# End of layer 1's cross attention: three operations change engine or place

## The chip, the cores and the metric

One Trainium2 chip; the kernel runs on one of its cores. The metric is the device time of one execution in microseconds (us). The core's engines work side by side, each on a queue of its own: PE (TensorE: matrix products and transposes through PSUM), DVE (VectorE), ACT (ScalarE), POOL (GpSimd) and SP, which here only issues transfers. An engine takes its instructions in order; where one needs the result of another engine, it waits, and everything behind it in that queue waits too.

## The reference

Two decoder layers on 32 sequences of 100 tokens of 256 values in float32, each layer with self attention, cross attention to a context of 361 positions of 192 values, and a feed-forward part. The change lies where layer 1's cross attention ends and its mixture of experts begins:

```python
# cross attention of layer 1
q = xn @ Wq
kv = context @ Wkv
...
dots = jnp.where(mask, dots, -jnp.inf)
attn = jax.nn.softmax(dots, axis=-1)
out = jnp.einsum('bhnm,bhmd->bhnd', attn, v)
...
return out @ Wo + bo
# experts of layer 1, on x_flat = rows of _layernorm(x)
shared = jnp.einsum('td,dh->th', jax.nn.silu(shared), shared_w2.T)
gate_logits = x_flat @ gate_w.T
top_k_gates, top_k_idx = jax.lax.top_k(gate_logits, TOP_K)
...
expert_out = jnp.einsum('teh,edh->ted', jax.nn.silu(h), experts_w2)
selected = jnp.einsum('ted,te->td', expert_out, gates)
return (shared + selected).reshape(B, S, D)
x = x + _L1_ffn_ref(_layernorm(x, axis=-1), ...)
```

## The kernel before

The 32 sequences are taken in 8 groups of 4 (`NG`, `G`). The cross attention works in 128 units (`NU`): unit u is one sequence with four of its 16 heads. For a unit, `scores` makes the products of queries and keys, DVE adds the mask and takes the row's extreme, `exponentials` lets ACT evaluate Exp (one instruction of 100x361 a head, with the row sums), and `divided` takes the reciprocal of the four row sums on DVE and multiplies all four heads' weights by it on POOL (100x1444 in one instruction, line 2369). `turn_weights` transposes the weights on PE in three chunks of the context positions, four heads a chunk; ACT copies the first and the third chunk from PSUM and DVE the second. `sums` multiplies them with the values on PE, and DVE copies the result into `oT`.

The order is written out by hand: `two_turns(n)` runs units n and n+1 in the stage of `turn_weights` and `sums`, while later units' values, keys, scores and exponentials are put between. Within `in_order()` the queues of PE, DVE, ACT and POOL follow that order exactly; SP's does not. Two units ahead, `half_of(n)` divides unit n+1. For the last pair, n = 126, nothing is left to put between: unit 127 is divided in `half_of(126)`, and then follow both units' transposes, both units' sums, and `finish` of the last group (the output projection of `oT`, bias on DVE for one half at line 147 and on ACT for the other at line 142, transposes back at line 2426, the residual sum on DVE at line 2433, transfer of the new rows to `x_dram`).

`gating` is the way of one group's rows into the experts, in parts: part 0 the statistics of the layer norm on DVE with a power and a product on POOL (lines 168 to 183, in `stats`), part 1 the norm itself in place, four ACT instructions of 100x256 (`scaled`, line 199), part 2 the transposes of the normed rows (line 217) and a copy of them to `xT_dram`, then logits, the two largest, gates and places. For groups 0 to 6 the parts are spread over the units of the next group (`norms_of`, `part_of`). The rows of a group then go to `sorted_dram`, one indirect transfer on POOL for each of two experts and each sequence (`send`, line 2280, called by `sends`): those of group 6 are issued from unit 124 on, two behind each pair of units and four at the end. All of them write the same tensor.

The last group has no next one. Behind the attention the stage of the shared expert opens, with PE, DVE, ACT and SP in written order and POOL's left to the scheduler. POOL first fills small tables and an empty block (lines 2560 to 2573). SP stores the empty block (2727, 2728) and loads rows and earlier sums (2627, 2637). The last group's parts 0 and 1 stand ahead of the loop over units (h, m): 256 tokens by 128 hidden columns. A turn n of the loop is `hidden(h, m)` (product with the first matrix on PE, line 230, then Silu on ACT, line 2651) and `added` of the unit two turns back (product with the second matrix, line 2659). Parts 2, 3 to 6, 7 and 8 for the last group come in turns 4, 8, 12 and 14; part 6 has an Exp.

PSUM has four tiles called mm, taken in turn by every `mm_tile()`, and two called sc. `ACT_TABLE_LOAD` is in no line of the kernel: it stands ahead of an ACT function that is not in the table at work. `half` is a constant tile filled with 0.5.

Of the kernel before, what the change touches and what calls it, by code (L numbers as in the profile page):

```python
# [10 lines left out]
F32 = mybir.dt.float32  # L11
# [3 lines left out]
AF = mybir.ActivationFunctionType  # L15
ALU = mybir.AluOpType
# [50 lines left out]
def kernel(ctx: ExitStack, tc: tile.TileContext, io: dict, out: bass.AP):  # L67
# [53 lines left out]
    def bc(ap, axis, n):  # L121

        ap = ap.unsqueeze(axis)
        shape = list(ap.shape)
        shape[axis] = n
        return ap.to_broadcast(shape)
# [68 lines left out]
    def scaled(dst, src, n, sh_rs, np_=T):  # L195

        sh, rs = sh_rs
        for i in range(n) if isinstance(n, int) else n:
            nc.scalar.activation(
                dst[:, i, :], src[:, i, :], AF.Identity, bias=sh[:np_, i : i + 1],  # L200
                scale=rs[:np_, i : i + 1],
            )
# [627 lines left out]
    with tc.tile_pool(name="x0", bufs=2) as pool, tc.tile_pool(name="x0p", bufs=1) as fixed:  # L830
# [158 lines left out]
        def exponentials(b, c, e):  # L989

            if c == 0 and e == 0:
                exs[b] = (
                    pool.tile([T, XH, NK], F32, tag="ex", name="ex"),
                    small.tile([T, XH], F32, tag="sm4", name="sm4"),
                )
            ex, sm = exs[b]
            if e == 0:
                shifted[0] = (
                    pool.tile([T, 2, NK], F32, tag="s", name="s"),
                    small.tile([T, 2], F32, tag="nmx", name="nmx"),  # L1000
                )
            s, nmx = shifted[0]
            ps = scs[b, c] if e == 0 else scs.pop((b, c))
            nc.vector.tensor_tensor_reduce(
                s[:, e, :], ps[e][:T, :NK], mbuf[b % 2], 1.0, 3.4e38, ALU.add, ALU.min,
                nmx[:, e : e + 1],
            )
            nc.scalar.activation(
                ex[:, 2 * c + e, :], s[:, e, :], AF.Exp, bias=nmx[:, e : e + 1], scale=-1.0,
                accum_out=sm[:, 2 * c + e : 2 * c + e + 1],  # L1010
            )
# [1185 lines left out]
    def gating(pool, g, part):  # L2197

        own = slice(g * G, (g + 1) * G)
        if part == 0:  # L2200
            gated[g] = stats(xs[g], G, tag="n", shift=True)
        elif part == 1:
            scaled(xs[g], xs[g], G, gated[g])
        elif part == 2:
            gT = pool.tile([P, 2, GT], F32, tag="lnT", name="gT", bufs=1)
            transposed(gT, xs[g], tiles=mm_tile)
            nc.sync.dma_start(xT_dram[:, :, g * GT : (g + 1) * GT], gT)
            gated[g] = gT
        elif part == 3:
            gated[g] = logits(w5, wg, gated[g])  # L2210
        elif part == 3.5:
            lg = small.tile([T, G, E], F32, tag="lg", name="lg")
            nc.vector.tensor_copy(lg, logits_back(gated[g]))
            gated[g] = lg
        elif part == 4:
            gated[g] = largest(gated[g], range(2))
        elif part == 5:
            top, hots = largest(None, range(2, G), gated[g])

            df = small.tile([T, G], F32, tag="df", name="df")  # L2220
            nc.vector.tensor_tensor(df, top[:T, :, 1], top[:T, :, 0], ALU.subtract)
            gated[g] = df, hots
        elif part == 6:
            df, hots = gated[g]
            nc.scalar.activation(df, df, AF.Exp)

            hs = w5.tile([T, G, E], F32, tag="hs", name="hs", bufs=2)
            hc = w5.tile([T, G + 1, E], F32, tag="hc", name="hc", bufs=2)
            nc.vector.tensor_tensor(hs, hots[:T, 0], hots[:T, 1], ALU.add)
            nc.vector.memset(hc[:, 0], 0.0)  # L2230
            for i in range(G):
                nc.vector.tensor_tensor(hc[:, i + 1], hc[:, i], hs[:, i], ALU.add)
            hh = w5.tile([T, 2, G, E], F32, tag="hh", name="hh", bufs=2)
            nc.vector.tensor_copy(hh, hots[:T])
            nc.gpsimd.iota(
                xrows[g][:, :, D + E : ROW].bitcast(I32), pattern=[[T, G], [0, 1]],
                base=g * GT, channel_multiplier=1,
            )
            gated[g] = df, hots, hs, hc, hh
        elif part == 7:  # L2240
            df, hots, hs, hc, hh = gated[g]
            g0 = small.tile([T, G], F32, tag="g0", name="g0")
            nc.vector.tensor_scalar_add(g0, df, 1.0)
            nc.vector.reciprocal(g0, g0)
            g1 = small.tile([T, G], F32, tag="g1", name="g1")
            nc.vector.tensor_tensor(g1, df, g0, ALU.mult)
            gates = xrows[g][:, :, D : D + E]
            nc.vector.tensor_tensor(gates, hots[:T, 0], bc(g0, 2, E), ALU.mult)
            nc.vector.tensor_tensor(hots[:T, 1], hots[:T, 1], bc(g1, 2, E), ALU.mult)
            nc.vector.tensor_tensor(gates, gates, hots[:T, 1], ALU.add)  # L2250
        else:

            df, hots, hs, hc, hh = gated.pop(g)
            pl = mm_tile()
            n = G * E
            nc.tensor.matmul(
                pl[:, :n], before[:, 0, :], hs.rearrange("p i e -> p (i e)"),
                start=True, stop=False,
            )
            nc.tensor.matmul(  # L2260
                pl[:, :n], before[:, 1, :], hc[:, :G].rearrange("p i e -> p (i e)"),
                start=False, stop=True,
            )
            nc.tensor.matmul(
                pl[:, n : n + E], before[:, 1, :], hc[:, G], start=True, stop=True
            )
            at = w5.tile([T, G, E], F32, tag="at", name="at", bufs=2)
            nc.vector.tensor_tensor(
                at, pl[:T, :n].rearrange("p (i e) -> p i e", e=E), bc(base[:T], 1, G), ALU.add
            )  # L2270
            nc.vector.tensor_tensor(base, base, pl[:, n : n + E], ALU.add)
            pf = w5.tile([T, 2, G], F32, tag="pf", name="pf", bufs=2)
            for k in range(2):
                nc.vector.tensor_tensor(hh[:, k], hh[:, k], at, ALU.mult)
                nc.vector.tensor_reduce(pf[:, k, :], hh[:, k], AX.X, ALU.add)
            nc.vector.tensor_copy(pos[:, :, own], pf)
# [9 lines left out]
    with tc.tile_pool(name="x1", bufs=2) as pool:  # L2286
# [78 lines left out]
        def divided(u):  # L2365
            ex, sm = exs[u]
            rc = small.tile([T, 4], F32, tag="rc4", name="rc4")
            nc.vector.reciprocal(rc, sm)  # L2368
            nc.gpsimd.tensor_tensor(ex, ex, bc(rc, 2, S2), ALU.mult)  # L2369

        def turn_weights(ex):
# [118 lines left out]
        def half_of(n):  # L2490

            if n == 4:
                loaded.extend(load_expert(0))
            if n >= 0 and n % 4 == 0 and n // 4 + 2 < B:
                cTs[n // 4 + 2] = context(n // 4 + 2)
            if n >= 0:
                part_of(n)
            v, last = n + 2 - n % 2, n % 2 == 1
            if v < NU:
                if not last:  # L2500
                    vbs[v // 2] = value_tiles()
                values(v, last, 0)
            if n + 3 < NU:
                keys(n + 3, 0)
            if -1 <= n and n + 1 < NU:
                divided(n + 1)
            if n >= 0:
                norms_of(n)
            if v < NU:
                values(v, last, 1)  # L2510
            if n + 2 < NU:
                scores(n + 2, 0)
                exponentials(n + 2, 0, 0)
            if n + 3 < NU:
                keys(n + 3, 1)
            if n + 2 < NU:
                exponentials(n + 2, 0, 1)
                scores(n + 2, 1)

        def two_turns(n):  # L2520

            half_of(n)
            for e in range(2):
                if n >= 0:
                    eTs[n + e] = turn_weights(exs.pop(n + e)[0])
                if n + 2 < NU:
                    exponentials(n + 2, 1, e)
            half_of(n + 1)
            for e in range(2):
                if n + 3 < NU:  # L2530
                    exponentials(n + 3, 1, e)
                if n >= 0:
                    u = n + e
                    if u % 16 == 0:
                        oTs[u // 16] = pool.tile([P, 8, GT], F32, tag="oT", name="oT", bufs=1)
                    sums(u, eTs.pop(u), vbs[u // 2], oTs[u // 16])
                    sends(u)
# [459 lines left out]
```

## Time and profile before

| | us |
|---|---|
| runs | 3261.96, 3264.95, 3269.97 |
| median of the runs | 3264.95 |
| profiled execution | 3261.03 |
| its span, first to last instruction | 3259.3 |
| its mean granted clock of PE | 0.985 |
| first unit's weights divided by POOL | 1509.9 |
| last unit's weights divided by POOL | 2657.7 |
| shared expert's first hidden product | 2678.9 |
| experts' first transposes | 2863.9 |

A row of the timeline gives start, duration, engine, line, operation, what is written and from what, shapes, how many instructions are merged, and in brackets how long the engine had been idle and what ended that. PEld is the loading of weights into PE, beside its products. A float32 product shows as two rows of PE. "PEclk" is the granted clock of PE as a share of full speed.

The places of the change in the profiled execution:

| line | engine | what | x | us |
|---|---|---|---|---|
| 2369 | POOL | weights times reciprocal, 100x1444 | 128 | 2.59 each |
| 199 | ACT | norm of a group's rows, 100x256 | 32 | 0.59 each, four of the last group 2.07 together |
| 2651 | ACT | table load | 2 | 1.28 each |
| 2225 | ACT | table load | 1 | 1.28 |

### The profile page before, as it was taken

The page shows a single profiled execution, that of the slowest core. Times are in us where ns is not written, and L with a number is a line of the kernel's source. Part 1 is how long each engine was busy: PE and PEld are TensorE (multiplying, and loading weights), DVE is VectorE, ACT ScalarE, POOL GpSimd, SP SyncE. Part 2 cuts the span into 40 slices and gives each one's busy share as a digit, 9 for nine tenths or more (in the row PEclk, how much of TensorE's full clock was granted, in tenths as well). Part 3 has the DMA queues.
Part 4 walks back from the last instruction along what each step waited for, and adds up shares of the span by engine and source line. Part 5 has one row for each costly group of instructions (what it writes and reads, how often), then busy time and mean ns, then how long its engine had stood idle before and what let it go on. Part 6 is the DMA issues. An engine that isn't in the chain of part 4 may idle for free. (4 is left out here: it accounts for less than half of the span.)

```text
span 3259.3 us, 66468 instructions
## 1 busy us (share of the span) xinstructions
PE 3139.3 (96%) x25174; PEld 2136.5 (66%) x25174; DVE 1822.3 (56%) x5220; ACT 1643.6 (50%) x3725; POOL 1333.2 (41%) x1192
## 2 busy tenths in 40 slices
PE   8998999989998899999999999999999989999998
PEld 6775666656666643335666666666666658899998
DVE  6777666757897578876455546464655541011111
ACT  5665666666775467775545445454545432211111
POOL 3445888875776522201333333333343332012222
PEclk9999999999998999999999999999999999999999
DMA  9502211101013722101000101000010013466665
GB/s 298 167 16 56 56 51 52 49 11 51 25 33 87 222 63 54 31 1 38 18 20 13 35 15 30 20 21 24 17 35 13 24 41 102 133 183 182 187 183 152
DMA packets 165701, 228.73 MB, mean 70 GB/s; under 512 B 22846, under 2 KB 139618, under 8 KB 164998
## 3 DMA queue, kind: packets, MB, share of 16 engines
q1 hardware_dynamic: 133592, 185.22, 18.3%
q0 software_dynamic: 20304, 27.99, 4.1%
q10 hardware_dynamic: 11486, 11.23, 1.0%
q8 instruction: 205, 3.36, 0.4%
q14 instruction: 114, 0.93, 0.1%
HBM read 150.92 MB, written 73.41 MB: 69 GB/s over the span
## 5 line engine op out<-in xcount | busy, mean ns | idle before, releaser
L2369 POOL TENSOR_TENSOR ex<-ex,rc 100x1444 f32<-100x1444 f32 x128 | 332.0, 2594 | 693.8 <-DVE rc L2368 445.0
L2360 ACT ACTIVATE ex<-s,nmx 100x361 f32<-100x361 f32 x512 | 305.7, 598 | 116.1 <-DVE nmx L2351 116.1
L403 POOL TENSOR_TENSOR s<-s,nmx 100x800 f32<-100x800 f32 x128 | 197.9, 1547 | 198.0 <-DVE nmx L402 175.7
L1962 ACT ACTIVATE h<-sc,cols 128x800 f32<-128x800 f32 x256 | 222.5, 924 | 95.3 <-PE sc L1956 95.2
L2828 POOL DMA_INDIRECT out_x<-y,xg x53 | 83.0, 1566 | 425.7 <-DVE y L2827 249.3
L2351 DVE CUSTOM_DVE_ANT_0 s<-sc,mb 100x361 f32<-100x361 f32 x512 | 250.7, 528 | 7.6 <-PE sc L2344 7.6
L2810 ACT ACTIVATE hgT<-sc 128x1024 f32<-128x1024 f32 x53 | 54.3, 1024 | 326.5 <-PE sc L230 326.5
L2827 DVE TENSOR_SCALAR y<-mm,gx 128x256 f32<-128x256 f32 x53 | 25.7, 484 | 323.4 <-PE mm L230 323.4
L230 PE MATMUL sc<-xgT,w1b 128*128 128x128 f32 x1696 | 198.1, 275 | 0.4 <-DVE xgT L2795 0.4
L2344 PE MATMUL sc<-kT,qT 64*100 64x361 f32 x1024 | 197.6, 463 | 0.0
L230 PEld LDWEIGHTS sc<-xgT,w1b 128*128 128x128 f32 x1696 | 193.6, 192 | 0.7 <-DVE xgT L2795 0.6
L230 PE MATMUL mm<-wx,hgT 128*128 x848 | 191.6, 379 | 0.0
L2316 PE MATMUL mm<-x_wa,cT 128*128 128x512 f32 (+1 forms) x512 | 191.4, 496 | 0.1
L2332 DVE COPY vb<-mm 128x512 f32<-128x512 f32 x64 | 44.3, 692 | 252.6 <-PE mm L2321 252.6
L2376 PEld LDWEIGHTS mm<-ident,ex 100*128 100x128 f32 (+1 forms) x1536 | 144.9, 152 | 52.3 <-issue 31.3
L1900 PE MATMUL mm<-cT,x_wa 128*128 128x361 f32 x512 | 176.3, 467 | 0.0
L2376 PE MATMUL mm<-ident,ex 100*128 100x100 f32 (+1 forms) x1536 | 168.7, 260 | 5.7 <-POOL ex L2369 5.1
L181 POOL TENSOR_TENSOR rs<-va,neghalf 100x4 f32<-100x4 f32 (+1 forms) x95 | 92.4, 975 | 194.5 <-DVE sh L180 87.8
L230 PEld LDWEIGHTS mm<-wx,hgT 128*128 128x128 f32 x848 | 157.2, 190 | 19.2
L2394 PEld LDWEIGHTS mm<-eT,vb 128*64 128x64 f32 (+1 forms) x3072 | 135.9, 137 | 33.6 <-issue 33.6
L408 ACT ACTIVATE ex<-s 100x800 f32<-100x800 f32 x128 | 111.5, 871 | 91.8 <-POOL s L403 88.3
L2394 PE MATMUL mm<-eT,vb 128*64 128x100 f32 (+1 forms) x3072 | 148.5, 252 | 0.0
(435 smaller groups left out, 7229.8 us busy)
## 6 DMA issues: line engine op xcount, KB each, us to landing
w1b<-in_f_w SPq DMA_DIRECT2D x55, 1024.0 KB
rows_dram<-zero SPq DMA_DIRECT2D x32, 896.0 KB
cT<-in_ctxT SPq DMA_DIRECT2D x64, 180.5 KB
cT<-in_ctxT SPq DMA_DIRECT2D x128, 90.2 KB
xg<-rows_dram SPq DMA_DIRECT2D x65, 128.0 KB
y_dram<-y ACTq DMA_DIRECT2D x65, 128.0 KB
wx<-in_f_w SPq DMA_DIRECT2D x8, 1024.0 KB
xg<-sorted_dram SPq DMA_DIRECT2D x57, 132.5 KB
```

The costliest lines, as they stand in the source:

```text
L230: nc.tensor.matmul(ps, lhsT[k], rhs[k], start=(k == 0), stop=(k == n - 1))
L403: nc.gpsimd.tensor_tensor(sm, sm, bc(nmx, 2, T), ALU.add)
L408: nc.scalar.activation(ex, sms.pop((s, hf)), AF.Exp, scale=0.25)
L1900: nc.tensor.matmul(kTs[u][c][:, :S2], x1_wa[:, m * P : (m + 1) * P], cT[:, 0, :], start=True, stop=False,)
L1962: nc.scalar.activation(h1, both[r2][:, :, :GT], AF.Tanh, bias=col("a1_b1", o))
L2316: nc.tensor.matmul(ps[e][:kn, :n], cT[:, 0, at], x1_wa[:, 1024 + c0 : 1024 + c0 + n], start=True, stop=False,)
L2344: nc.tensor.matmul(ps[:T, e, :S2], qT[p0 : p0 + 64, m, tok], kT[p0 : p0 + 64, c, :], start=True, stop=True,)
L2351: nc.vector.tensor_tensor_reduce(s[:, e, :], ps[:T, e, :S2], mb, 1.0, 3.4e38, ALU.add, ALU.min, nmx[:, e : e + 1],)
L2360: nc.scalar.activation(ex[:, 2 * c + e, :], s[:, e, :], AF.Exp, bias=nmx[:, e : e + 1], scale=-1.0, accum_out=sm[:, 2 * c + e : 2 * c + e ...
L2369: nc.gpsimd.tensor_tensor(ex, ex, bc(rc, 2, S2), ALU.mult)
L2376: nc.tensor.transpose(pt[:kn, j * T : (j + 1) * T], ex[:, j, k0 : k0 + kn], ident[:T, :T])
L2394: nc.tensor.matmul(po[64 * e : 64 * e + 64, m * T : (m + 1) * T], vb[k][:kn, v0 + 64 * h : v0 + 64 * h + 64] if k < 2 else vb[2 + u % 2][: ...
```

## The change

It has three parts.

- In `gating` part 1, for the last group alone, four DVE tensor_scalar (times `rs`, plus `sh`) take the place of the four ACT instructions of `scaled`.
- In `divided`, for unit 127 alone, four DVE tensor_scalar of 100x361 (a head each, times its reciprocal) take the place of the one POOL multiply.
- In `two_turns(124)`, the two exponentials of unit 127 that stood one ahead of each unit's sums both stand ahead of both, and behind them ACT evaluates Silu on one element of `half` into a new tile of the pool `small`.

```diff
         elif part == 1:
-            scaled(xs[g], xs[g], G, gated[g])
+            if g == NG - 1:
+                sh, rs = gated[g]
+                for i in range(G):
+                    xi = xs[g][:, i, :]
+                    nc.vector.tensor_scalar(
+                        xi, xi, rs[:T, i : i + 1], sh[:T, i : i + 1], ALU.mult, ALU.add
+                    )
+            else:
+                scaled(xs[g], xs[g], G, gated[g])
...
             nc.vector.reciprocal(rc, sm)
+            if u == NU - 1:
+                for j in range(4):
+                    nc.vector.tensor_scalar(
+                        ex[:, j, :], ex[:, j, :], rc[:, j : j + 1], None, ALU.mult
+                    )
+                return
             nc.gpsimd.tensor_tensor(ex, ex, bc(rc, 2, S2), ALU.mult)
...
             half_of(n + 1)
+            if n + 4 == NU:
+                for e in range(2):
+                    exponentials(n + 3, 1, e)
+                first_silu = small.tile([1, 1], F32, tag="silu", name="silu", bufs=1)
+                nc.scalar.activation(first_silu, half[0:1, 0:1], AF.Silu)
             for e in range(2):
-                if n + 3 < NU:
+                if n + 4 < NU:
                     exponentials(n + 3, 1, e)
```

## The prediction

> **What bounds the kernel now.** I read the page first, then the waits and the stretches around the end of the cross attention, then the timeline engine by engine. On the page PE is nearly always busy:
>
> ```profile
> PE 3139.3 (96%) x25174; PEld 2136.5 (66%) x25174; DVE 1822.3 (56%) x5220; ACT 1643.6 (50%) x3725; POOL 1333.2 (41%) x1192
> ```
>
> The chain of waits that ended last covers only the final 14 us, so I looked for the places where PE stands still. Between 2655 and 2700 us the waits (engine, waited for, us, times, longest) hold three of PE:
>
> ```profile
> PE sc L2659 <- ACT hT L2651: 6.3, 1, 6.3
> PE mm L2376 <- POOL ex L2369: 5.1, 1, 5.1
> PE mm L2426 <- ACT yT L142: 0.6, 1, 0.6
> ```
>
> The stretches (us, PE busy, PEld, DVE, ACT, POOL, PEclk, DMA share, GB/s) show what follows each long wait: PE restarts at half clock.
>
> ```profile
> 2655.20:2660.30 5.10, 0.00 (x0) 0.00 (x0) 0.24 (x1) 0.49 (x1) 3.59 (x2) 0.88 0.11 34
> 2660.30:2662.60 2.30, 2.25 (x14) 2.08 (x14) 0.57 (x1) 0.49 (x1) 1.02 (x1) 0.50 0.14 38
> 2662.60:2666.40 3.80, 3.80 (x50) 3.67 (x49) 0.37 (x1) 0.49 (x1) 0.99 (x1) 0.57 0.05 13
> ...
> 2681.70:2687.90 6.20, 0.01 (x1) 0.01 (x1) 0.91 (x5) 3.80 (x7) 1.24 (x2) 0.87 0.86 273
> 2687.90:2690.00 2.10, 2.10 (x5) 1.74 (x6) 0.00 (x0) 0.49 (x2) 0.00 (x0) 0.50 0.64 225
> 2690.00:2693.20 3.20, 3.20 (x9) 2.48 (x9) 0.00 (x0) 0.38 (x1) 0.00 (x0) 0.51 0.00 0
> ```
>
> The timeline says who is late. First hole: DVE has the reciprocal at 2654.55, but POOL sends rows before it multiplies.
>
> ```profile
> 2653.51 1.02 POOL L2280 DMA_INDIRECT sorted_dram<-x,pos  x1 [0.18 <-issue]
> 2654.37 0.18 DVE L2368 RECIPROCAL rc<-sm 100x4 f32<-100x4 f32 x1
> 2656.68 0.99 POOL L2280 DMA_INDIRECT sorted_dram<-x,pos  x1 [2.14 <-DMA sorted_dram<-x,pos]
> 2657.69 2.60 POOL L2369 TENSOR_TENSOR ex<-ex,rc 100x1444 f32<-100x1444 f32 x1
> ```
>
> Second hole: ACT sits on the last group's norm until POOL has the power, then loads a table, then does the first Silu, which PE needs for its first product with the second matrix.
>
> ```profile
> 2678.87 2.76 PE L230 MATMUL mm<-xT_first,w 128*128 128x256 f32 x12
> ...
> 2682.72 1.04 POOL L181 TENSOR_TENSOR rs<-va,neghalf 100x4 f32<-100x4 f32 x1 [2.50 <-DVE sh L180]
> 2683.83 0.20 POOL L183 TENSOR_TENSOR sh<-sh,rs 100x4 f32<-100x4 f32 x1
> 2684.07 2.07 ACT L199 ACTIVATE x<-x,sh,rs 100x256 f32<-100x256 f32 x4 [6.06 <-POOL sh L183]
> 2686.16 1.28 ACT L2651 ACT_TABLE_LOAD   x1
> 2687.45 0.94 ACT L2651 ACTIVATE hT<-mm 128x256 f32<-128x256 f32 x3
> ...
> 2687.89 2.08 PE L2659 MATMUL sc<-w,hT 128*128 128x256 f32 x4 [6.27 <-ACT hT L2651]
> ```
>
> Behind 2693 us PE is busy and at clock 1.00 in every stretch up to 3200 us, so what PE gains here should reach the end.
>
> **Division on VectorE.** Removed: the POOL multiply of unit 127 (2.60 us) and its place behind two sends. Added: four tensor_scalar of 100x361 on DVE. The trace has none; the nearest rows are four of 100x256 from SBUF in 1.38 us (line 190, at 273.64) and the 128x361 copy out of PSUM (line 2299, 529 ns, starting every 0.45 us), four of which take 1.88. Mine is SBUF to SBUF with more columns than the first, so I take 1.55. They start behind the reciprocal at 2654.52 and end at 2656.07 (2655.9 to 2656.4). Queued behind them on DVE is the copy of unit 126's middle turned chunk (0.57), done at 2656.6 instead of 2655.4; its PSUM tile is, four tiles round, the one for unit 127's third chunk, whose turn comes after two others of about 0.4 each, from 2656.6. PE ended unit 126's transposes at 2655.20 and now waits some 0.9 us in pieces. Full-clock durations: 12 transposes 1.28 (at 2653.92) against 2.30 here, 48 products 2.29 (at 2651.70) against 3.85. Sum: 5.14 wait, + 1.02 and + 1.56 of half clock, - 0.8 for the new waits = **6.9 us** (6.5 to 7.1). The output projection then starts near 2659.5 instead of 2666.36.
>
> **One Silu behind the last exponential.** The exponentials of unit 127 are already back to back on ACT (2653.01 and 2653.59), so writing them ahead of the sums moves nothing. Added at 2654.27: a table load (1.28, as at 2686.16) and a one-element Silu. A small ACT copy takes 173 ns (line 136, 128x16) and the 100x4 Exp takes 201; I take 0.25. Queued behind: ACT's copy of unit 126's first turned chunk, which moves from 2654.58 to about 2655.8, done 2656.3. Its tile serves unit 127's second chunk, which cannot begin before the division ends (2656.07) plus 0.1: at most 0.2 us, inside the 0.8 above. Removed: the load ahead of the first hidden Silu. With the norm off ACT, that load would run in ACT's idle time anyway: ACT is done with line 142 at 2678.00 and the first hidden product at 2679.9, 1.9 us for a load of 1.28. So this edit alone is worth 0 (-0.3 to 0).
>
> The trace puts the load at 1.28 us, with Silu following at 2687.45 at once. [...]
>
> **Norm on VectorE.** Removed from ACT: four Identity of 100x256 (2.07). Added: four DVE tensor_scalar of the same shape (1.38, line 190). DVE waits for POOL ahead of them; behind them in its queue stand only the copy of the turned rows (which needs them) and the first add into the sums, line 2666, 18 PE groups later. ACT now goes from line 142 straight to the hidden Silus. The first is ready 2678.87 + 1.03 + 0.1 + 0.38 = 2680.4 on the old scale, before PE has its three first hidden products out (2681.6): no wait. Wait saved 6.27. Half clock saved: from 2687.89 to the transposes at 2694.90 PE needs 7.01 for five groups, which start 0.865 apart at full clock (2696.48, 2697.34), 4.33: 2.7. Together 9.0.
>
> **What is late next.** PE reaches those transposes of the normed rows at 2685.8 - 6.9 = 2678.9. The power is on POOL, behind eight sends, each waiting for the landing of the one before. Where sends follow each other so in this stage, 25 of 30 steps are 3.0 to 3.5 us from start to start, five 3.7 to 4.3. From 2653.51, seven steps of about 3.2 give the last at 2675.9, over at 2676.9 (before: 2677.9). Then the seven small POOL instructions of lines 2560 to 2573 (0.96 from first to last), the power and product (1.31 with the gap), four norms (1.38) and hops of 0.1: 2680.7. The last row is wanted at 2679.2: a new wait of **1.5 us** (0.5 at steps of 3.05). SP is held too: lines 2727 and 2728 wait for POOL's empty block, till about 2678, and behind them the loads of rows and sums (3.3 us of issues); the first add that wants them, 2705.5 now, comes near 2691.
>
> **Sum.** 6.9 + 9.0 - 1.5 = 14.4 us off the profiled execution: 3261.03 - 14.4 = 3246.6, span 3244.9. Its time was 3.9 below the median of the runs, so I set the forecast against the median: 3264.95 - 14.4 = **3250.5**. Its own bounds: gain 12 to 16, and runs 3 us under to 5 us over their median: 3246 to 3258.
>
> **Rivals.**
> (1) POOL's sends set the pace. For: their chain is 23 us, does not shift with PE, and PE now arrives 7 us sooner. Against: 25 of 30 steps. At 4.1 each step the last send ends at 2683.2, rows at 2687.0, a wait of 7.8; past some 4 us the clock falls (0.88 and 0.87 in the holes above) and costs about 2.7: gain 5, time 3260.
> (2) The table is lost again: if line 142's Identity is not in Silu's set, the change does not do what it says; one load goes ahead of line 142, where PE waits (+1.28), another ahead of the first hidden Silu, covered as above. For: no Identity follows a Silu in this trace. Against: Copy does (line 136 at 2695.79, no load behind it). Gain 13.1, time 3252.
> (3) Given back: a later stage does not start earlier because a transfer holds it. Against: the shared expert's rows (line 2543) were loaded at 1850, and wx2 and w1b are issued as PE moves on. Gain 0 to 3, time 3263.
> (4) Slower: the new small tile shifts addresses and the 55 loads of w1b (1 MB) get slower. They fill 0.63 of the DMA share from 2900 to 3200 while PE takes 7.24 us a block (2869.37 to 2876.62 starts). 53 blocks lose 384 x (0.63f - 1): with a factor f of 1.65 the loss is 15 and the gain gone, at 1.75 the time is 3290. Against: those tiles lie in a pool on the right side, the new one is in the first pool on the left.
>
> **Chances.** Forecast 0.70, (1) 0.13, (2) 0.05, (3) 0.06, (4) 0.06. A measurement here tells about 0.3%, 9.8 us, from no change. Faster by more: 0.95 of the forecast, a third of (1), most of (2): 0.75. Within: the rest of these and (3): 0.19. Slower: 0.06. The range 3244 to 3262 holds the forecast with its spread, (1) and (2); what of (3) and (4) is outside is some 0.1.
>
> **What would show it.** Right: PE's first hole under 1.5 us and no stretch at clock 0.5 before 3200; the wait of line 2659 for hT gone; a new PE wait of 0.5 to 3 us at line 217 whose chain goes back to POOL; three table loads behind 2650 as now, the first near 2654 and none at line 142. Wrong: a wait of PE for ACT's copies near 2657, or a hole over 4 us at line 217, or a gap growing after 2700.

## The result and the profile after

The changed kernel took 3253.45 us (median of 6 runs, 3251.18 to 3255.91), the kernel before 3265.33 beside it (median of 6, 3260.72 to 3269.97): a ratio of 0.9964, 95% interval 0.9951 to 0.9977, so 0.36% less, 11.9 us. Its profiled execution took 3252.98, with a span of 3251.3.

The spans differ by 8.0 us only, because this execution came to the end of the attention 3.6 us later (unit 126's transposes at 2657.48, before at 2653.92) in code that is the same. I therefore measure all traces from the start of unit 126's transposes. To the transpose of the logits in turn 8 (line 248) it was 49.61 us before (to 2703.53) and is 37.94 now (to 2695.42): **11.67 us gained**. To the experts' first transposes it was 210.00 (2863.92) and is 198.31 (2855.79): nothing is given back behind.

First, PE's waits between 2655 and 2700 us in the changed kernel (engine, waited for, us, times, longest):

```profile
PE mm L217 <- DVE x L2207: 2.1, 1, 2.1
PE mm L2440 <- ACT yT L142: 0.6, 1, 0.6
PE mm L248 <- ACT lT L242: 0.4, 1, 0.4
```

Both long waits of before are gone, and a new one is at the transposes of the normed rows. Its stretches (us, PE busy, PEld, DVE, ACT, POOL, PEclk, DMA share, GB/s):

```profile
2675.00:2682.40 7.40, 7.40 (x38) 6.32 (x36) 3.90 (x14) 1.92 (x5) 3.20 (x8) 1.00 0.28 84
2682.40:2684.60 2.20, 0.11 (x2) 0.02 (x1) 0.48 (x2) 0.00 (x0) 1.60 (x6) 1.00 0.36 113
2684.60:2686.40 1.80, 1.77 (x8) 1.29 (x9) 1.22 (x4) 0.00 (x0) 0.00 (x0) 0.65 0.61 96
2686.40:2688.50 2.10, 2.10 (x7) 1.75 (x6) 0.25 (x1) 0.49 (x1) 0.00 (x0) 0.50 0.90 309
2688.50:2700.00 11.50, 11.14 (x65) 9.08 (x64) 3.81 (x27) 4.93 (x10) 0.00 (x0) 1.00 0.40 137
```

PE stands still for 2.1 us, and behind that it again runs at half clock, until about 2688.5; that is a sign which the prediction had named as not to come. The timeline of the first seam, from ACT's last Exp on:

```profile
2657.84 1.28 ACT L2547 ACT_TABLE_LOAD   x1
2657.93 0.18 DVE L2376 RECIPROCAL rc<-sm 100x4 f32<-100x4 f32 x1
2658.14 1.36 DVE L2379 TENSOR_SCALAR ex<-ex,rc 100x361 f32<-100x361 f32 x4
2659.14 0.20 ACT L2547 ACTIVATE silu<-half 1x1 f32<-1x1 f32 x1
2659.24 1.23 ACT L2397 COPY eT<-mm 128x400 f32<-128x400 f32 x3
...
2660.69 2.30 PE L2408 MATMUL mm<-eT,vb 128*64 128x100 f32 x48
2662.92 11.01 PE L230 MATMUL mm<-oT,x_wo 128*128 128x400 f32 x32
```

The four multiplies take 1.36 us, and the 48 products run at full clock (2.30 us; the granted clock is 1.00 from 2657.40 to 2682.40). From unit 126's transposes to the projection it is 5.44 us, before 12.44. POOL, in the same timeline:

```profile
2663.10 0.99 POOL L2288 DMA_INDIRECT sorted_dram<-x,pos  x1 [2.05 <-DMA sorted_dram<-x,pos]
2668.59 0.99 POOL L2288 DMA_INDIRECT sorted_dram<-x,pos  x1 [4.50 <-issue]
...
2680.84 0.99 POOL L2288 DMA_INDIRECT sorted_dram<-x,pos  x1 [2.13 <-DMA sorted_dram<-x,pos]
2681.85 0.20 POOL L2579 IOTA ti<- 128x57 int32 x1
...
2682.76 1.04 POOL L181 TENSOR_TENSOR rs<-va,neghalf 100x4 f32<-100x4 f32 x1
2683.88 0.20 POOL L183 TENSOR_TENSOR sh<-sh,rs 100x4 f32<-100x4 f32 x1
2684.12 1.38 DVE L2207 TENSOR_SCALAR x<-x,rs,sh 100x256 f32<-100x256 f32 x4 [4.86 <-POOL sh L183]
2684.58 2.07 PE L217 MATMUL mm<-ident,x 100*128 100x100 f32 x8 [2.09 <-DVE x L2207]
```

Read upwards from PE: it waits for the norm, the norm for POOL's product, the power for nothing but its place in POOL's queue, behind eight sends and the seven small instructions that follow them (0.9 us). DVE had the statistics at 2679.25.

### The profile page after: what moved, and what is told of

Read it like the earlier page. It is cut to its first block, busy times and chain, and to the rows that moved or that the text cites. A ratio compares the mean times of both kernels' runs of the same rounds, so it can differ in the third digit from the quotient of the medians.

```text
span 3251.3 us, 66466 instructions
## 1 busy us (share of the span) xinstructions
PE 3141.0 (97%) x25174; PEld 2138.2 (66%) x25174; DVE 1824.8 (56%) x5228; ACT 1642.2 (51%) x3722; POOL 1331.5 (41%) x1191
## 5 line engine op out<-in xcount | busy, mean ns | idle before, releaser
L2340 DVE COPY vb<-mm 128x512 f32<-128x512 f32 x64 | 44.2, 691 | 252.6 <-PE mm L2329 252.6
L2408 PEld LDWEIGHTS mm<-eT,vb 128*64 128x64 f32 (+1 forms) x3072 | 134.4, 136 | 33.5 <-issue 33.4
```

The lines of the kernel that those rows point to most:

```text
L2408: nc.tensor.matmul(po[64 * e : 64 * e + 64, m * T : (m + 1) * T], vb[k][:kn, v0 + 64 * h : v0 + 64 * h + 64] if k < 2 else vb[2 + u % 2][: ...
```

## The experiments

There are eight experiments on two chips. Beside experiments 1 to 4 the kernel before had a median of 3275.4 us (21 runs, 3269.8 to 3284.2), beside 5 to 8 one of 3267.04 (9 runs, 3264.8 to 3273.8). The spread of the runs arises for the most part ahead of the seam: unit 126's transposes start anywhere from 2653.9 to 2666.9 us in the ten traces. The table therefore gives the us from the start of those transposes to four points of the kernel, from PE's timeline.

| kernel | projection | first hidden product | logits' transpose | experts |
|---|---|---|---|---|
| before | 12.4 | 25.0 | 49.6 | 210.0 |
| changed | 5.4 | 17.9 | 37.9 | 198.3 |
| 1 divide alone | 5.9 | 18.4 | 44.2 | 205.7 |
| 2 norm alone | 12.7 | 25.2 | 41.2 | 201.6 |
| 3 changed, no early Silu | 5.9 | 18.4 | 38.5 | 198.9 |
| 4 changed, late sends | 5.9 | 18.4 | 34.0 | 194.4 |
| 5 early Silu alone | 12.7 | 25.2 | 47.5 | 207.9 |
| 6 changed, transposes in turn 6 | 5.4 | 17.9 | 33.5 | 193.9 |
| 7 changed again | 5.4 | 18.0 | 37.9 | 198.3 |
| 8 late sends again | 5.4 | 18.0 | 33.5 | 193.9 |

Rows 4 and 8 are one kernel and differ by 0.5 in the first column, so less than 0.6 us there says nothing.

**1. The division alone.** The kernel before with this:

```diff
+            if u == NU - 1:
+                for j in range(4):
+                    nc.vector.tensor_scalar(
+                        ex[:, j, :], ex[:, j, :], rc[:, j : j + 1], None, ALU.mult
+                    )
+                return
             nc.gpsimd.tensor_tensor(ex, ex, bc(rc, 2, S2), ALU.mult)
```

> Of the change only the division on VectorE. Theory (POOL's chain of sends does not move with PE): the first hole closes and PE reaches the first hidden products 6.9 us sooner, but the norm on ACT still waits for POOL's power, which stands behind the sends and comes only some 3 us sooner; the second hole grows from 6.3 to 9 to 11 us, and the gain is 2 to 4 us against the kernel before. Rival (the parts add up): second hole 6.3 as before, gain 6.9.

Measured: 5.5 us gained in the stretch; ratio 0.9990 (0.9981 to 0.9999), median 3272.79. The medians are 2.6 us apart, and their interval of 0.3 to 6.2 us cannot tell 5.5 from the 2 to 4 expected; the trace decides. PE's timeline:

```profile
2665.40 1.88 PE L2382 MATMUL mm<-ident,ex 100*128 100x100 f32 x12 [0.62 <-DVE ex L2371]
...
2693.16 2.07 PE L2665 MATMUL sc<-w,hT 128*128 128x256 f32 x4 [8.47 <-ACT hT L2657]
```

The second hole grew from 6.27 to 8.47, as the theory said and the rival did not, though less than its 9 to 11; and behind it PE was at full pace again sooner (5.9 us from there to the normed rows' transposes at 2699.04, before 7.0): two groups of four products are slow there, 2.07 and 1.58 us, and three before, 2.08, 1.91 and 1.87, where the ones behind them take 1.03. The gain is outside both ranges: the mechanism stands, its size was too pessimistic.

**2. The norm alone.** The kernel before with the new branch of `gating` part 1 only:

```diff
+            if g == NG - 1:
+                sh, rs = gated[g]
+                for i in range(G):
+                    xi = xs[g][:, i, :]
+                    nc.vector.tensor_scalar(
+                        xi, xi, rs[:T, i : i + 1], sh[:T, i : i + 1], ALU.mult, ALU.add
+                    )
+            else:
+                scaled(xs[g], xs[g], G, gated[g])
```

> Of the change only the norm on VectorE. Theory: the first hole stays (5.1 us and half clock); the second goes, for the table load falls into ACT's idle time ahead of the first hidden product; PE is late enough for the normed rows, wait at line 217 under 0.5 us; gain 9 us. Rival (the load must be taken out of the way too): the second hole keeps 1 to 1.5 us, gain under 8.

Measured: 8.4 us in the stretch, 8.7 of it behind the first hidden product (16.0 to the logits, before 24.7); ratio 0.9964 (0.9954 to 0.9975). ACT's timeline:

```profile
2690.70 0.59 ACT L142 ACTIVATE yT<-mm,cols 128x400 f32<-128x400 f32 x1 [14.65 <-PE mm L230]
2693.34 1.28 ACT L2659 ACT_TABLE_LOAD   x1 [2.04 <-DVE x L2441]
2694.63 0.94 ACT L2659 ACTIVATE hT<-mm 128x256 f32<-128x256 f32 x3
```

The load is not free of waits: it starts 2.04 us behind line 142, not at once. The profile names DVE's residual sum as what released it. I take it for a wait for the first hidden product, which the Silu behind the load reads and which ends 0.15 us before the load starts (2692.16 + 1.03 = 2693.19); the profile does not name that wait. It still costs PE only 0.15 us (its wait for hT in this trace; 6.27 before), because PE has three hidden products to make first. At line 217 PE does not wait.

**3. No early Silu.** The changed kernel with `two_turns` as it was before.

> The changed kernel without its early Silu. Theory: the early load is worth nothing once the norm is off ACT; same time as the changed kernel within 0.5 us in the trace, the load running after line 142 while ACT waits for the first hidden product. Rival: the load is paid ahead of the first hidden Silu, 1.3 us slower, with a wait of PE for hT.

Measured: behind the first hidden product 20.1 us to the logits, 20.0 in the changed kernel; PE waits 0.15 for hT. The whole stretch is 0.6 longer, but that stands in its first column, where one kernel differs by 0.5. The median 3256.86 (ratio 0.9949, 0.9935 to 0.9962) lies in the same range as the changed kernel's. The early Silu is worth some 0.1 us here.

**4. The sends later.** The changed kernel with this:

```diff
-            for n in range(NU, NU + 4):
-                sends(n)
...
+            if n == 10:
+                for m in range(4, 8):
+                    at = send((NG - 2) * G + m // 2, m % 2)
+                    if not sent:
+                        tc.keep_in_program_order(at)
+                    put(at)
             if n == 18:
                 blocks_of()
```

> The changed kernel with the last four sends of group 6 taken out of the end of the attention and issued in turn 10 of the shared expert's loop, behind the power. Theory (the wait at line 217 is POOL's chain of sends): that wait, 2.1 us, and the half clock behind it go, 4.4 us faster than the changed kernel, about 16 under the kernel before. Rival (statistics, power and norm are themselves too long for PE's new pace): the wait stays at 2 us, same time as the changed kernel.

Measured: 34.0 us to the logits, 15.6 less than before and 4.0 less than the changed kernel. POOL's and PE's timelines:

```profile
2686.49 0.14 POOL L2590 IOTA empty<- 128x1 int32 x1
2689.12 1.04 POOL L181 TENSOR_TENSOR rs<-va,neghalf 100x4 f32<-100x4 f32 x1 [2.49 <-DVE sh L180]
```

```profile
2691.32 1.03 PE L2676 MATMUL sc<-w,hT 128*128 128x256 f32 x4
2692.19 0.85 PE L217 MATMUL mm<-ident,x 100*128 100x100 f32 x8
2692.88 1.05 PE L230 MATMUL mm<-xT_first,w 128*128 128x256 f32 x4
```

POOL now waits for DVE's statistics instead of the other way round, and PE goes through line 217 without a wait: the rival is out. The median (3258.26, ratio 0.9954, 0.9940 to 0.9968) cannot show the 4 us beside that of experiment 3 (3256.86), so the kernel is run again in 8.

**5. The early Silu alone.** The kernel before with the changed `two_turns`.

> Of the change only the early Silu (and the two exponentials written ahead of the sums). Theory: the early table load falls into ACT's idle time behind the last exponential, and the first hidden Silu starts right behind the norm; the second hole shrinks from 6.3 by 1.3 to 5.0 us, the rest stays; from unit 126's transposes to the transpose of the logits 48.3 us where the kernel before has 49.6. Rival (the load costs more there, for ACT's copies come late): the first hole grows and the sum is 49.6 or more.

Measured (one run, 3259.35, so the trace alone counts): 47.5 us to the logits, 2.1 gained. PE's wait for hT fell from 6.27 to 4.84, as expected; the other 0.7 us is what is left of a quicker way behind it (6.11 us from there to the normed rows' transposes at 2693.18, before 7.01) and 0.2 lost ahead of it (25.2 to the first hidden product, before 25.0). The first hole is 4.99. So the early load is worth 2 us as long as the norm is on ACT, and some 0.1 with it on DVE.

**6. The transposes two turns later.** The changed kernel with this:

```diff
-            if n in (4, 8, 12, 14):
-                for part in {4: (2,), 8: (3, 3.5, 4, 5, 6), 12: (7,), 14: (8,)}[n]:
+            if n in (6, 8, 12, 14):
+                for part in {6: (2,), 8: (3, 3.5, 4, 5, 6), 12: (7,), 14: (8,)}[n]:
```

> The changed kernel with the transposes of the normed rows in turn 6 of the loop, not 4; the sends as in the changed kernel. Theory (PE has only come too early for rows that POOL's queue delays, and the work of two turns, 3.5 us, covers it): no wait at line 217, no half clock behind it, from unit 126's transposes to the transpose of the logits 34.0 us as with late sends (37.9 in the changed kernel). Rival (the logits in turn 8 then come too early for the copies of the turned rows): a new wait at line 237 takes the place of the old, 36 us or more.

Measured: 33.5 us; median 3247.88 of 5 runs, ratio 0.9936 (0.9923 to 0.9950). No new wait at line 237:

```profile
2690.09 0.86 PE L217 MATMUL mm<-ident,x 100*128 100x100 f32 x8
...
2694.36 0.55 PE L237 MATMUL mm<-gT,f_wg 128*32 128x100 f32 x16
2695.27 0.32 PE L248 MATMUL mm<-ident,lT 128*100 128x128 f32 x1 [0.36 <-ACT lT L242]
```

Its profiled execution took 3257.46, the longest of its five: the end behind the experts' first transposes was 400.1 us against 395.4 to 395.5 in the kernels before and changed, with one POOL wait of 5.5 us for a store to the output. The other four runs took 3247.2 to 3249.9.

**7 and 8. The changed kernel and the late sends once more**, unedited, beside 6 on one chip.

> The changed kernel, unedited, beside the other two on one chip: from unit 126's transposes to the transpose of the logits 37.9 us again, wait at line 217 between 1.5 and 2.5 us; median 4 us over the two others, if the medians can tell that much.

> The kernel with late sends once more, for a median beside the changed kernel's on one chip: the same stretch 34.0 us, median 4 us under the changed kernel's. If the medians are apart by less than 1, the 4 us are given back behind the stretch or drowned by the spread of the runs; the trace's start of the experts' first transposes tells which.

Measured: 37.9 and 33.5 us, the wait at line 217 1.95 us in the changed kernel, medians 3256.96 (ratio 0.9964, 0.9951 to 0.9978) and 3250.50 (0.9945, 0.9931 to 0.9959), 6.5 apart, where the traces have 4.4. The stretches around line 217, first the changed kernel, then the late sends:

```profile
2685.10:2687.20 2.10, 0.20 (x1) 0.00 (x0) 0.42 (x2) 0.00 (x0) 1.57 (x5) 1.00 0.35 109
2687.20:2689.00 1.80, 1.72 (x8) 1.20 (x9) 1.23 (x4) 0.00 (x0) 0.00 (x0) 0.73 0.59 96
2689.00:2691.00 2.00, 2.00 (x7) 1.64 (x7) 0.31 (x1) 0.49 (x1) 0.00 (x0) 0.50 0.89 306
```

```profile
2684.30:2686.40 2.10, 2.10 (x17) 1.88 (x15) 0.57 (x1) 0.69 (x2) 1.49 (x3) 1.00 1.05 375
2686.40:2693.00 6.60, 6.24 (x44) 5.07 (x43) 0.00 (x0) 1.62 (x6) 1.52 (x2) 1.00 0.58 208
```

The hole and the half clock behind it are repeated in the one and absent in the other. Kernels 6 and 8 beat the kernel before clearly. Against the changed kernel the traces show 4.4 us for each; of the times, all five of kernel 8 and four of the five of kernel 6 lie under all five of the changed one, though the intervals of 7 and 8 overlap a little. Between 6 and 8 the intervals do not decide.

## Why the prediction was right, and where it was off

The direction and most of the size came out: 14.4 us were forecast, 11.7 are in the trace and 11.9 in the medians; the median, 3253.45, is 3 us over the forecast 3250.5. The medians' interval, 7.5 to 16.0 us, holds both 11.7 and 14.4, so what follows rests on the traces.

- **Division, 6.9 us forecast.** 7.0 measured to the projection (12.44 to 5.44). The four instructions took 1.36, just under the lower of the two rows I had set as bounds (1.38). The waits and the half clock behind them went as summed: the 24 transposes took 3.28 where 24 without waits at a granted clock of 1.00 have 2.62 (at 2006.74 in the kernel before), so 0.7 of new waits where 0.8 had been put.
- **Early Silu, 0 (-0.3 to 0).** About 0.1 in its favour (experiment 3). The load took the 1.28 of the row, and load and Silu follow each other at 2657.84 and 2659.14, 1.30 apart. One assumption in the working was wrong without weight: left at its old place, the load does not run the moment ACT is free; in experiments 2 and 3 it starts 2.04 us later, 0.15 and 0.14 behind the end of the first hidden product, and PE waits 0.15 for the result because it has three such products to make first.
- **Norm, 9.0 us.** 8.7 alone (experiment 2), and 9.1 where nothing else is late: from the first hidden product to the logits 24.66 before, 15.53 with late sends.
- **What is late next, -1.5 us.** This term was mis-sized: it is -4.5 (24.66 - 20.00 = 4.66 gained in place of 9.13). The mechanism is the one named: experiments 4, 6 and 8, which take four of the eight sends away or give PE other work, remove it whole. Two things made it larger. The last send started at 2680.84, which is 2677.3 on the scale of before, not 2675.9, because one step between sends was 5.5 us, beyond the 4.3 that the trace before had shown at the same place, from the third to the fourth send. And I let the clock fall only past some 4 us of standing still, where here it fell behind a hole of 2.1 us: of the 4.5 some 2.1 are the hole and the rest is waiting in pieces and half clock. (A slip without weight: by its own terms the working has PE at the transposes 0.1 later than the 2685.8 that it starts from.) With this term right the sum would have been 7.0 + 9.1 - 4.5 = 11.6.
- **Rivals.** (1), POOL's sends set the pace, is what happened in part, between the forecast and its price of a 7.8 us wait. (2) did not come: in the changed kernel line 142 at 2673.97 and the first hidden Silu at 2676.61 have no load ahead of them. (3) did not come: the stretch behind the logits is 160.4 us in both. (4) did not come: from the experts' first transposes to the end it is 395.4 and 395.5. What a shifted address does to a load was my assumption, and no run shows it.

The three parts alone gain 5.5, 8.4 and 2.1, together 16.0, and jointly only 11.7: what the early Silu gains alone, 2.1, the norm gains too (0.1 is left with both), and the division makes PE arrive ahead of POOL's queue.

## What to carry to other kernels

When a stall on the busy engine is removed, list every other chain that does not move with it and compare its end with the new arrival: here POOL's sends, which had cost nothing at line 217 before, took back 4.5 of 16 us. Such a wait can be covered by two turns of other work as well as removed; moving one number from 4 to 6 was worth as much as rearranging the sends. Price an edit in the company it will have: the early table load is worth 2 us with the norm on ACT and 0.1 without.

## What had not been expected of the hardware

In the changed kernel PE's clock fell behind a hole of about 2 us, and it fell while PE was already at work again. PE stops at 2682.5, starts the transposes at 2684.58, and the half clock begins at 2685.1, 2.6 us after PE stopped. The 5.1 us hole before had let it fall 3.8 us after PE stopped (2655.20 to 2659.03). In experiment 3 a hole of 1.5 us (from 2684.1) let it fall 3.7 us after PE stopped, at 2687.8, when PE was through the transposes and back at products. Another place of the changed kernel shows the same, where a wait of 2.15 us ends in transposes:

```profile
1137.00:1138.20 1.20, 0.00 (x0) 0.00 (x1) 0.53 (x2) 0.00 (x0) 1.00 (x3) 1.00 0.91 279
1138.20:1139.00 0.80, 0.75 (x3) 0.41 (x3) 0.80 (x3) 0.00 (x0) 0.80 (x1) 0.93 0.69 209
1139.00:1139.50 0.50, 0.43 (x3) 0.27 (x3) 0.50 (x2) 0.00 (x0) 0.30 (x3) 0.50 0.55 143
```

Transposes alone did not bring it: in the kernel before, PE does nothing but transposes from 2006.74 to 2010.33, 3.6 us, and the clock stays at 1.00 there and behind.

Beside the length of a hole, the clock records of the traces of the kernel before and the changed one show this: in each of the two, all changes of the granted clock lie a whole number of steps of 3.41 us apart (to 0.01 us), and half clock lasts one to four steps, apart from a last stretch that runs past the end of the kernel. These are the step with the hole and the one behind it in the changed kernel, then the step of transposes alone in the kernel before:

```profile
2681.71:2685.12 3.41, 1.30 (x6) 0.63 (x4) 1.00 (x4) 0.38 (x1) 2.28 (x10) 1.00 0.34 109
2685.12:2688.54 3.42, 3.40 (x12) 2.82 (x12) 0.95 (x3) 0.53 (x2) 0.00 (x0) 0.50 0.79 211
```

```profile
2007.10:2010.51 3.41, 3.30 (x33) 2.86 (x32) 2.46 (x9) 3.41 (x11) 0.00 (x0) 1.00 0.02 5
```

PE is busy for 0.38 of the step with the hole and for 0.97 of the one with transposes alone. In the kernel before, the half clocks from 2659.03 and from 2686.34 each stand behind a step in which PE is not busy at all. In experiment 7 the 3.41 us ahead of the half clock, which begins at about 2688.0, have some 0.42, in experiment 3 some 0.63. In the two traces of before and changed, up to 3231 us, half clock follows 32 of the 1838 steps at full clock: in those PE is busy for 0.00 to 0.73 of the step, in the others for 0.48 or more. What decides where the two overlap stays open.

The step from the third of the eight sends to the fourth, with no releaser shown, is 4.27 to 4.31 us in the kernel before and experiments 1 and 2, and 5.49, 5.75 and 6.49 in the changed kernel and experiments 3 and 4, which have both the division and the norm on VectorE; the other steps between sends that follow each other there are 3.0 to 3.8. In four of these six traces (changed, 1, 3 and 4) one packet of instructions of 0.02 MB was loaded within that wait, in two it was not; the cause stays open.
